# Quarter weights in partition order, and the second token tile and first mask on ScalarE's queue, in the ramp of a block-sparse gated layer

## Chip, cores and metric

One core of a Trainium2 chip. The time is device microseconds of one execution; lower is better. The kernel before has a median of 439.04 us over three runs (438.39 to 439.83).

## What is computed

The input x holds 2 batches of 1024 tokens with 1024 features, in float32. Each token is normalised over its features, without scale or shift. The normalised tokens go through two products with 1024 x 1024 matrices: `s`, with a weight of which only those 32 x 32 blocks count whose integer mask has a positive sum, plus a bias; and `g`, a dense weight plus a sum of eight low-rank products whose coefficients per batch are a softmax of scores against eight keys, followed by SiLU. The result is `x + s * g`.

```python
bm = mask.reshape(Nb, BH, Kb, BW).sum(axis=(1, 3)) > 0
w = (weight.reshape(Nb, BH, Kb, BW) * bm[:, None, :, None]).reshape(N, K)
s = einsum('bsk,nk->bsn', xn, w) + bias
delta = einsum('be,bser,ero->bso', coeffs, einsum('bsi,eir->bser', xn, lora_down), lora_up)
g = silu(einsum('bsi,oi->bso', xn, W_org) + delta)
out = x + s * g
```

## The kernel before

Products are made in three float32r passes on PE (TensorE): every operand is split into a high part and the remainder (`_hi`, `_lo`), and high by high, high by low and low by high are added up in PSUM (lines 456, 459 and 460). For the first batch, tokens lie on the partitions of the result in eight tiles of 128; the weights lie in `slot` tiles of 512 columns, the tokens in `xgrp`. The second batch is computed with a scheme of seven block products (line 1395) from sums of blocks that are prepared meanwhile.

What matters here is the ramp, the first 25 us or so, in which nothing is in SBUF. To begin early, it works with a quarter of the columns of the sparse weight (256 of 1024, `NQ`) and token tile by token tile. The order of the work of PE, DVE (VectorE), ACT (ScalarE) and POOL (GpSimd) is written out by hand, in a block with `manual_schedule`: what is written first is issued first on each of these engines, and each of them works strictly in that order. DMAs are issued by the queue of the engine that is named, here `nc.sync` (SP, SyncE) for all loads of the ramp, in the order written.

The loads and their tiles:
- `x_load(i)`: token tile i, 128 rows of 4 KB. Tile 0 (`acc`) comes in two halves of 2 KB per row, tiles 1 to 3 (`raw`) and 4 to 7 (`xlate`) whole.
- `mask_load(q)`: two transfers of 512 KB into `ramp`, the mask of quarter q in an order in which four partitions hold one block row.
- `w_load(q, k0)`: four of the eight row blocks of the quarter weights, 512 KB, into `ramp`.

The work on PE's way to its first real product is this:
- `warm_up(13)`: filler matmuls (`warm`, line 676) that depend on no data.
- `x_stats`, `rstd_of`, `shift_of`: mean and variance of tile 0 by halves on DVE (line 149), the power on POOL (line 157), the shift on DVE (line 163); `x_norm_half`: normalisation on ACT (line 167).
- `x_turn(0, 0)`, `x_turn(0, 1)`: eight transposes on PE (`pt`, line 210).
- `warm_up(12)`: twelve more fillers.
- Meanwhile on DVE, in this order: statistics of tile 1, the sum over the mask's first half (line 257), the sum over half of the mask's second half, with the other half on ACT (line 255), the join (line 261) and the spread (line 265).
- `mask_apply_mm(0)`: eight tiny matmuls (`mp`, line 275) that expand the block mask; then the weights are multiplied by it (`w_mul`, line 590, on DVE and POOL), split (`w_hi` on ACT, line 593, `w_lo`, line 597), and the products begin (line 456).

The first loads are written so:

```python
x_load(0, 2)
x_load(1)
mask_load(0)
w_load(0, 0)
w_load(0, 4)
x_load(2)
mask_load(1)
```

Of the kernel before, what the change touches and what calls it, by code (L numbers as in the profile page):

```python
# [17 lines left out]
P = 128  # L18
# [4 lines left out]
NH = 512  # L23
NQ = 256
# [8 lines left out]
def kernel(  # L33
# [11 lines left out]
    wq: bass.AP,  # L45
    wu: bass.AP,
    biasT: bass.AP,
    out: bass.AP,
):

# [10 lines left out]
    nc = tc.nc  # L61
# [75 lines left out]
    def nat_tile(dt=F32):  # L137
        k = turns[0] % 3
        turns[0] += 1
        v = raw_flat[:, k * D : (k + 1) * D]  # L140
        return v if dt == F32 else v.bitcast(dt)
# [420 lines left out]
    mh = [ramp[:, q, :, :].bitcast(I32) for q in range(2)]  # L562
    wh = [ramp[:, 2 + q, :, :].rearrange("p a (k n) -> p (a k) n", n=NQ) for q in range(2)]
    xr = [acc[0]] + [nat_tile() for _ in range(3)]
# [3 lines left out]
    sums = {}  # L568
    squares = {}

    def x_load(i, parts=1):
        n = D // parts
        for h in range(parts):
            nc.sync.dma_start(xr[i][:, h * n : (h + 1) * n], x[i * P : (i + 1) * P, h * n : (h + 1) * n])

    def mask_load(q):
        for c in range(2):
            nc.sync.dma_start(mh[q][:, c, :], mask[2 * q + c])

    def w_load(q, k0):  # L580
        nc.sync.dma_start(
            wh[q][:, k0 : k0 + 4, :],
            wT[k0 * P : (k0 + 4) * P, q * NQ : (q + 1) * NQ].rearrange("(k p) n -> p k n", p=P),
        )

    def w_mul(q, k0, eng, n=2):

# [65 lines left out]

    with tc.manual_schedule(engines={mybir.EngineType.PE, mybir.EngineType.DVE, mybir.EngineType.Activation, mybir.EngineType.Pool}):
        x_load(0, 2)
        x_load(1)
        mask_load(0)
        w_load(0, 0)
        w_load(0, 4)
        x_load(2)  # L660
        mask_load(1)
        x_load(3)
        w_load(1, 0)
        w_load(1, 4)
        nc.sync.dma_start(bias_bc, bias.partition_broadcast(P))
# [838 lines left out]
        close(cm_t, cm_o0, cm_t2, cm_g, cm_o1)  # L1504


_ORDER = ["x", "xT", "mask", "wT", "bias", "worgT", "down", "up", "keysT", "wq", "wu", "biasT"]


def _layout(inputs):  # L1510
    import numpy as np

    a = {k: np.asarray(v) for k, v in inputs.items()}
    x = a["L0_attn_data"].reshape(B * S, D)

    mask = a["L0_attn_mask"].reshape(8, 4, 32, 32, 32).transpose(0, 3, 1, 2, 4).reshape(8, P, D)

    down = (
        a["L0_ffn_lora_down"].transpose(0, 2, 1).reshape(4, P, NKT, P).transpose(2, 1, 0, 3)
    )  # L1520
    return {
        "x": x,
        "xT": x.T,
        "mask": mask,
        "wT": a["L0_attn_weight"].T,
        "bias": a["L0_attn_bias"],
        "worgT": a["L0_ffn_W_org"].T,
        "down": down,
        "up": a["L0_ffn_lora_up"].reshape(E_ * R_, D),
        "keysT": a["L0_ffn_lora_keys"].T,  # L1530
        "wq": a["L0_ffn_Wq"],

        "wu": a["L0_attn_weight"].T.reshape(2, 4, P, 2, 4, P).transpose(4, 2, 3, 0, 1, 5).reshape(4, P, 16 * P),
        "biasT": a["L0_attn_bias"].reshape(NKT, P).T,
    }


# [23 lines left out]
```

## Time and profile before

| | |
|---|---|
| Median of three runs | 439.04 us (438.39 to 439.83) |
| The profiled execution | 439.54 us, span 437.8 us |
| PE busy | 430.3 us, 98% of the span |
| DVE, ACT, POOL busy | 305.2, 184.6, 78.9 us |
| Granted TensorE clock | 1.0 of full speed |
| DMA | 88.48 MB, mean 202 GB/s |
| SP's queue (q1) | 64.77 MB; ACT's queue (q10) 7.08 MB; POOL's (q0) 16.26 MB |

The span is what the profiler sees of the program; the execution's time has 1.7 us more around it. Busy times of PE come from records whose ends are modelled. A row of the timeline gives the start, the length, the engine, the line and what is written from what, and in brackets how long the engine had been idle and whose work ended that idle time. "L574" is line 574 of the kernel before.

### The profile page before, as it was taken

To read this page: it belongs to the slowest core of one execution; us is meant where nothing else is said; L and a number is where in the kernel's file an instruction comes from. 1 tells how busy PE (TensorE), PEld (TensorE's weight loads), DVE (VectorE), ACT (ScalarE), POOL (GpSimd) and SP (SyncE) were. 2 spreads that over 40 slices of the span, in tenths; PEclk is the share of its full clock that TensorE was granted. 3 is DMA by queue.
4 is the path that set the end of the run, shared out by engine and by line. 5 is a ranking of instruction groups with operands and counts; after the bars stand their busy time and mean duration, and the time that the engine had idled before them with its cause. 6 is when DMAs were issued, how large, how long until landed. Compare 5 with 4: busy or idle time off the path is not lost.

```text
span 437.8 us, 5768 instructions
## 1 busy us (share of the span) xinstructions
PE 430.3 (98%) x2029; PEld 358.2 (82%) x2029; DVE 305.2 (70%) x508; ACT 184.6 (42%) x312; POOL 78.9 (18%) x103
## 2 busy tenths in 40 slices
PE   7999999999999999999999999999999999999996
PEld 5899888888888878888888888788888888888885
DVE  5889977766626779888966978878647385374624
ACT  3787435354731222236333344466335233441510
POOL 3342210002320312143132130010020030002000
PEclk9999999999999999999999999999999999999999
DMA  7996706777796798994699876996292165228003
GB/s 255 389 349 208 218 25 222 231 248 218 261 273 190 240 281 287 322 331 144 187 267 290 247 212 178 360 257 186 66 199 96 52 140 149 96 50 206 34 1 121
DMA packets 46013, 88.48 MB, mean 202 GB/s; under 512 B 4624, under 2 KB 15136, under 8 KB 45984
## 3 DMA queue, kind: packets, MB, share of 16 engines
q1 hardware_dynamic: 30480, 64.77, 44.7%
q0 software_dynamic: 6624, 16.26, 16.1%
q10 hardware_dynamic: 8880, 7.08, 5.0%
q8 instruction: 16, 0.26, 0.2%
q14 instruction: 13, 0.11, 0.1%
HBM read 68.17 MB, written 19.93 MB: 201 GB/s over the span
## 4 chain that ended last, share of the span: by engine, by line
PE 84%; DMA 5%; issue 4%; DVE 2%; POOL 2%; ACT 1%; SPq 0%; ACTq 0%; POOLq 0%; DVEq 0%
PE acc_ps L1395 25%; PE acc_ps L460 11%; PE acc_ps L459 11%; PE acc_ps L456 11%; PE py L1395 10%; PE psv L1149 6%; PE psw L421 2%; PE psw L420 2%; PE psw L1149 2%; PE psw L422 2%; DMA stash<-in_x_dram 2%; DMA xs<-xv 1%; DMA raw<-xv 1%; PE warm L676 1%; DMA acc<-in_x_dram 1%
## 5 line engine op out<-in xcount | busy, mean ns | idle before, releaser
L1395 PE MATMUL acc_ps<-xw,ow 128*128 128x512 f32 (+1 forms) x492 | 112.2, 384 | 0.2 <-DVE xw L1220 0.2
L456 PE MATMUL acc_ps<-slot,xgrp 128*128 128x512 f32 (+1 forms) x288 | 106.6, 370 | 0.1
L1395 PEld LDWEIGHTS acc_ps<-xw,ow 128*128 128x128 f32 x492 | 90.8, 188 | 18.9 <-DVE xw L1220 0.6
L460 PE MATMUL acc_ps<-slot,xgrp 128*128 128x512 f32 (+1 forms) x288 | 105.6, 367 | 0.2 <-DVE xgrp L609 0.2
L459 PE MATMUL acc_ps<-slot,xgrp 128*128 128x512 f32 (+1 forms) x288 | 105.5, 366 | 0.2
L460 PEld LDWEIGHTS acc_ps<-slot,xgrp 128*128 128x128 f32 x288 | 54.3, 188 | 9.6 <-DVE xgrp L609 0.6
L459 PEld LDWEIGHTS acc_ps<-slot,xgrp 128*128 128x128 f32 x288 | 54.3, 189 | 9.4 <-DVE slot L438 0.5
L456 PEld LDWEIGHTS acc_ps<-slot,xgrp 128*128 128x128 f32 x288 | 54.3, 189 | 9.4 <-ACT slot L593 0.6
L1395 PE MATMUL py<-xw,ow 128*128 128x512 f32 x192 | 46.3, 389 | 0.0
L1395 PEld LDWEIGHTS py<-xw,ow 128*128 128x128 f32 x192 | 36.0, 188 | 7.5
L1263 DVE TENSOR_TENSOR ow<-raw,ow 128x1024 fp32r<-128x1024 f32 (+1 forms) x32 | 34.5, 1087 | 7.7 <-ACT ow L1262 7.5
L1262 ACT CAST ow<-raw 128x1024 fp32r<-128x1024 f32 (+1 forms) x32 | 29.5, 941 | 3.0 <-DVE raw L1256 1.8
L508 POOL DMA_DIRECT2D stash<-in_x_dram x16 | 14.4, 900 | 74.7 <-DVE stash L505 74.7
L1378 POOL DMA_DIRECT2D gate<-in_xT_dram x12 | 10.5, 908 | 94.0 <-DVE gate L1372 67.9
L430 ACT CAST slot<-wo 128x512 fp32r<-128x512 f32 x16 | 9.9, 619 | 37.3 <-DVE wo L427 32.9
L420 PE MATMUL psw<-cut,dhi 128*128 128x512 f32 x64 | 24.9, 389 | 0.0
L421 PE MATMUL psw<-cut,dhi 128*128 128x512 f32 x64 | 24.9, 389 | 0.0
L422 PE MATMUL psw<-cut,dlo 128*128 128x512 f32 x64 | 24.9, 389 | 0.0
L1439 DVE TENSOR_TENSOR py<-py,s 128x512 f32<-128x512 f32 x8 | 5.6, 698 | 27.3 <-ACT s L1402 27.3
L1256 DVE TENSOR_TENSOR raw<-raw 128x512 f32<-128x512 f32 x32 | 21.4, 688 | 0.8 <-DMA raw<-yu 0.3
L1248 DVE TENSOR_TENSOR raw<-raw,m_sb 128x1024 f32<-128x1024 f32 x8 | 9.7, 1221 | 16.3 <-DMA raw<-in_wu_dram 16.3
L505 DVE TENSOR_TENSOR stash<-stash,mine 128x512 f32<-128x512 f32 x16 | 11.1, 692 | 10.8 <-ACT mine L481 10.5
(211 smaller groups left out, 605.0 us busy)
## 6 DMA issues: line engine op xcount, KB each, us to landing
wo<-in_worgT_dram SPq DMA_DIRECT2D x24, 256.0 KB, 3.9
raw<-in_x_dram SPq DMA_DIRECT2D x11, 512.0 KB, 4.4
ds<-in_down_dram SPq DMA_DIRECT2D x16, 256.0 KB, 3.4
stash<-in_x_dram POOLq DMA_DIRECT2D x16, 256.0 KB, 5.1
raw<-in_wu_dram SPq DMA_DIRECT2D x8, 512.0 KB, 5.8
raw<-yu SPq DMA_DIRECT2D x8, 512.0 KB, 3.8
out_dram<-stash ACTq DMA_DIRECT2D x14, 256.0 KB, 4.1
misc<-xv SPq DMA_DIRECT2D x12, 256.0 KB, 5.0
```

What stands on the lines that cost most here:

```text
L420: nc.tensor.matmul(ps, lhsT=dhi[:, c, :], rhs=u[c][:, 0, :], start=c == 0, stop=False)
L421: nc.tensor.matmul(ps, lhsT=dhi[:, c, :], rhs=u[c][:, 1, :], start=False, stop=False)
L422: nc.tensor.matmul(ps, lhsT=dlo[:, c, :], rhs=u[c][:, 0, :], start=False, stop=c == 3)
L456: nc.tensor.matmul(ps, lhsT=xs[:, kt, 0, cols], rhs=w[:, kt, 0, wc], start=kt == 0, stop=False)
L459: nc.tensor.matmul(ps, lhsT=xs[:, kt, 0, cols], rhs=w[:, kt, 1, wc], start=False, stop=False)
L460: nc.tensor.matmul(ps, lhsT=xs[:, kt, 1, cols], rhs=w[:, kt, 0, wc], start=False, stop=kt == NKT - 1)
L508: nc.gpsimd.dma_start(res, x[at], accum_op=ALU.add)
L1149: nc.tensor.matmul(ps, lhsT=w[:, a, wl, c, :], rhs=u[:, ul, :], start=start and c == 0 and n == 0, stop=c == 1 and n == 2, skip_group_chec ...
L1256: nc.vector.tensor_tensor(raw[:, o], raw[:, a], raw[:, b], op)
L1262: nc.scalar.copy(o[:, a:b, 0], raw[:, a:b])
L1263: nc.vector.tensor_tensor(o[:, a:b, 1], raw[:, a:b], o[:, a:b, 0].bitcast(F32), ALU.subtract)
L1395: nc.tensor.matmul(ps, lhsT=o[:, a, wl, j, :], rhs=xw[j][:, m, xl, cols], start=start and j == 0 and k == 0, stop=j == 3 and k == 2, skip_ ...
```

## The change

A new input `wr` holds the first 512 columns of the sparse weight once more, laid out on the host so that a load of `w_load` reads one run of 4 KB for each partition; before, a partition's share came in four runs of 1 KB. The bytes are the same and go to the same places. `x_load` and `mask_load` get an argument for the issuing engine, and tile 1 and the two transfers of the first mask are issued by ACT's queue. They are the first three instructions on ACT. SP's queue holds, in this order, the two halves of tile 0, the two weight loads, tile 2 and everything behind it as before. The order of all other instructions on every engine is the same. Lines of the changed kernel behind the edits are two lower for the ramp.

```diff
-    def x_load(i, parts=1):
+    def x_load(i, parts=1, eng=nc.sync):
         n = D // parts
         for h in range(parts):
-            nc.sync.dma_start(xr[i][:, h * n : (h + 1) * n], x[i * P : (i + 1) * P, h * n : (h + 1) * n])
-
-    def mask_load(q):
+            eng.dma_start(xr[i][:, h * n : (h + 1) * n], x[i * P : (i + 1) * P, h * n : (h + 1) * n])
+
+    def mask_load(q, eng=nc.sync):
         for c in range(2):
-            nc.sync.dma_start(mh[q][:, c, :], mask[2 * q + c])
+            eng.dma_start(mh[q][:, c, :], mask[2 * q + c])
 
     def w_load(q, k0):
-        nc.sync.dma_start(
-            wh[q][:, k0 : k0 + 4, :],
-            wT[k0 * P : (k0 + 4) * P, q * NQ : (q + 1) * NQ].rearrange("(k p) n -> p k n", p=P),
-        )
+        nc.sync.dma_start(wh[q][:, k0 : k0 + 4, :].rearrange("p k n -> p (k n)"), wr[q, k0 // 4])
...
         x_load(0, 2)
-        x_load(1)
-        mask_load(0)
+        x_load(1, eng=nc.scalar)
+        mask_load(0, nc.scalar)
         w_load(0, 0)
         w_load(0, 4)
         x_load(2)
...
+        "wr": a["L0_attn_weight"].T[:, :NH].reshape(2, 4, P, 2, NQ).transpose(3, 0, 2, 1, 4).reshape(2, 2, P, 4 * NQ),
```

More of the change, by code (lines that the diff above doesn't have):

```diff
@@ L47 @@
     biasT: bass.AP,
+    wr: bass.AP,
     out: bass.AP,
@@ L1504 @@
         close(cm_t, cm_o0, cm_t2, cm_g, cm_o1)
-_ORDER = ["x", "xT", "mask", "wT", "bias", "worgT", "down", "up", "keysT", "wq", "wu", "biasT"]
+_ORDER = ["x", "xT", "mask", "wT", "bias", "worgT", "down", "up", "keysT", "wq", "wu", "biasT", "wr"]
 def _layout(inputs):
```

## The prediction

> **What bounds the kernel now.** I read the page's engine table first, then the waits of PE alone, then the chain of waits over the first 14 us, then the timeline of PE, DVE and ACT there, and last the DMA by windows. All times are microseconds from the start of the span.
>
> The engine table and the waits of PE (engine and line, what it waited for, total, times, longest):
>
> ```profile
> PE 430.3 (98%) x2029; PEld 358.2 (82%) x2029; DVE 305.2 (70%) x508; ACT 184.6 (42%) x312; POOL 78.9 (18%) x103
> ...
> PE pt L210 <- ACT acc L167: 1.5, 1, 1.5
> PE warm L676 <- DVE ones_r L97: 1.1, 1, 1.1
> PE acc_ps L460 <- DVE xgrp L609: 0.2, 1, 0.2
> PE acc_ps L1395 <- DVE xw L1220: 0.2, 1, 0.2
> ```
>
> PE is busy for 98% of the span and has only four waits that count. The longest, 1.5 us, is in front of the first transposes. After the ramp nothing makes PE wait more than 0.2 us, so whatever the change gains or loses before PE becomes continuous goes through to the end at its full size. Only the ramp has to be costed. Its chain of waits (start, length, what):
>
> ```profile
> 0.81 0.38 SPq L574
> 1.24 3.62 DMA acc<-in_x_dram
> 4.89 0.70 DVE st L149
> 6.10 0.58 POOL rstd L157
> 6.95 1.53 ACT acc L167 x2
> 8.52 0.66 PE pt L210 x4
> 9.18 2.75 PE warm L676 x12
> 11.93 0.30 PE mp L275 x8
> 12.47 0.43 DVE ramp L590
> 12.92 0.41 ACT slot L593
> ```
>
> The chain starts with the second half of the first token tile (x0, tile acc), lands at 4.86, and goes statistics, rstd, normalisation, transposes, twelve fixed filler matmuls, then the mask's expansion (mp). The mask comes in only at mp. The same stretch as instructions (start, length, engine, what, idle before and its releaser):
>
> ```profile
> 4.89 0.69 DVE L149 BATCH_NORM_STATS2 st<-acc 128x6 f32<-128x512 f32 x1 [0.67 <-DMA acc<-in_x_dram]
> 7.90 1.29 DVE L149 BATCH_NORM_STATS2 st<-raw 128x6 f32<-128x512 f32 x2 [0.99 <-DMA raw<-in_x_dram]
> 10.48 0.63 ACT L255 ACTIVATE ramp<-ramp 128x512 f32<-128x512 int32 x1 [1.38 <-DMA ramp<-in_mask_dram]
> 8.94 2.99 PE L676 MATMUL warm<-ones_r 128*128 128x512 f32 x12
> 12.47 0.75 DVE L590 TENSOR_TENSOR ramp<-ramp,mp 128x256 f32<-128x256 f32 x2 [0.53 <-ACT m_sb L282]
> ```
>
> So the landings are: x0's second half 4.86, the second tile (x1) 7.88, the mask's second half 10.46. The weights were there already when first used at 12.47: that wait ends on ACT, not on a DMA. DMA by windows (length, then the engines, granted clock, DMA share, GB/s):
>
> ```profile
> 1.80:3.50 1.70, 1.70 (x6) 1.32 (x5) 0.67 (x2) 0.00 (x0) 1.12 (x1) 1.00 0.92 288
> 3.50:6.00 2.50, 2.50 (x9) 1.96 (x7) 1.74 (x4) 1.28 (x1) 1.42 (x2) 1.00 0.83 165
> 6.00:7.90 1.90, 0.44 (x3) 0.09 (x2) 0.23 (x2) 0.95 (x2) 0.57 (x1) 1.00 0.99 379
> ```
>
> From 6 us on the DMA engines are full at 379 GB/s; before that there is a slow stretch of 165 GB/s. One queue, SP's, already fills them.
>
> **The change, part by part.**
>
> *Weights in 4 KB rows.* Four loads of 0.52 MB. The weight rows flow at 375 GB/s (10 to 12 us) and the 4 KB rows of x at 422 (14 to 15 us), so a load takes 1.40 against 1.24: 0.16 us less for each, two of them before the first product. Nothing on the path waits for weights, so 0 is taken. If that cover went, they would be worth 0.3.
>
> *Three issues on ACT.* SP's issues of 512 KB take 0.42 to 0.43 us, so ACT spends about 1.3. Its first work is a table load of 1.28 at 3.57, which waits for x0's first half, and after it ACT idles 2.10 before the normalisation. Cost 0; 1.3 without that cover.
>
> *Three issues off SP.* What is queued behind them on SP (weights, x2, the second mask) goes out about 1.3 us earlier. x2 is first read at 18.61 and the second mask at 19.17, neither after a wait for DMA, so no gain. SP's queue has eight completion counters in turn: the second mask's first load now waits for x1 instead of x0's first half; behind it on SP stand x3 and the second weights. In before mask loads took a median of 8.7 us from issue to landing, with all the loads ahead of them in the queue, so an issue up to 1.4 us later is hidden there. Cost 0.
>
> *x1 and the mask beside x0.* This is the price. ACT is free when PE and DVE are (first instructions at 1.12 and 0.90), so x1 is issued at about 0.9, before x0's second half (1.24). What two hardware queues do at once is seen at 126.8 to 127.4: a store that ACT issued at 123.96 stands beside SP loads issued at 121.88, 124.24 and 124.81.
>
> ```profile
> q10 hardware_dynamic: 75, 0.15, 65.6%
> q1 hardware_dynamic: 30, 0.07, 29.4%
> ```
>
> ACT's queue (q10) takes two thirds, SP's (q1) falls to less than one third, and the sum is no more than before. So I expect x1's 0.52 MB to be served between the two halves of x0. The lower bound of the delay of x0's second half is then 0.52 MB at 400 GB/s, 1.3 us. The upper one is x1's own landing in before: 1.05 MB were through at 7.88, and now x0's second half is last of the same 1.05 MB, 7.88 - 4.86 = 3.0 us. I take the middle, 2.1, because the slow stretch of 165 GB/s may or may not come back. Outside these bounds: if x0 keeps its place and the slow stretch goes, DVE's 0.67 of idle between the halves is gained (-0.7).
>
> At this place the Trainium skill speaks against the change: "DMA: Bandwidth & Descriptors", section "Issuing engines are not separate DMA queues", says that transfers from all issuers share the same 16 engines and interleave, so that a second issuer saves only sequencer time. The windows above agree (full at 379 GB/s from one queue). By the rule the delay is at least the 1.3; if ACT's queue brought bandwidth of its own, it would be none.
>
> *What the mask gives back.* In before PE stood 0.26 in front of mp, because the mask's sums ended at 11.82, 1.36 after its landing at 10.46. With x0 late, the fillers end late, and that 0.26 closes if the mask is there in time. In issue order x0a, x1, x0b, mask, weights, mask, 2.6 MB end with the mask's second half instead of 2.1: 0.52/0.39 = 1.3 us later, 11.8, sums done at 13.1. The fillers end at 11.5 + 2.1 = 13.6. The mask is not late, and PE's 0.26 is gained.
>
> *Sum:* + 2.1 - 0.26 = + 1.84 us at mp, and nothing behind mp has slack to take it back. The profiled execution took 439.54 (span 437.8 and 1.7 around it) and would take 441.4; the median of the runs shown is 0.5 lower, 439.04, so 440.9.
>
> **The rivals.** A difference of 0.3%, 1.3 us, is about what a measurement of this kernel can tell from no change.
>
> *A second loss on top.* Either the mask's second half also falls behind both weight loads (3.1 MB through instead of 2.1, at 0.39 MB/us 2.7 later: 13.2, sums at 14.5, mp 14.6 against 11.87: + 2.7), or PE loses its warm clock. For that: the opening thirteen fillers took 5.23, 0.40 each, the twelve at 8.94 took 2.99, 0.25 each, after an idle of 1.46; that idle grows to 3.6. Twelve at 0.40 cost 4.8 instead of 2.99, + 1.8 on 1.84 = + 3.7, 442.7. Against it: transposes stand between, and the granted clock is 1.00 throughout. The Trainium skill ("TensorE: Matmul & The Clock Gate", section "What's actually happening") puts the array back to half clock after an idle window of about 3.4 us; no idle so long is in this trace, and by the page 3.6 would be just enough.
>
> *Faster.* x0's halves keep their place (SP's two transfers are served before ACT's first) and the slow stretch, which follows on x1's first rows, no longer lies in x0's way. Then x0's second half lands by 4.2, and the chain gains 0.67 + 0.26 = 0.93: 438.1. It decides at a landing of x0 before 4.86 with the mask no later than 10.4. For it: ACT has never issued a DMA before 110 us, so its start is unseen. Against it: the 2.1 MB that end with the mask would have to pass with the weights beside them.
>
> *It makes no difference.* x0 late by 1.3 or less, without the slow stretch: + 1.0 or less, 439.0 to 440.0.
>
> **How the numbers follow.** The forecast (x0 behind x1) 0.48, of which 0.41 lie over + 1.3; the second loss 0.18; no difference 0.16; faster 0.18. The price of the faster case is only 0.2%. I still count 0.16 of its 0.18 as over 0.3%: the scatter of the runs (438.39 to 439.83) is as large, and one of PE's small waits of 0.2 lies in the ramp behind mp and may close too. So faster 0.16, slower 0.41 + 0.18 = 0.59, same 0.07 + 0.16 + 0.02 = 0.25. The range goes from the faster case, 438.1, to + 4.0, 443.0, a little over the second loss; it leaves out about 1 in 10 at each end. The likeliest case's own range is 440.0 to 441.7.
>
> **What would show it.** In the changed profile the second statistics of x0 should start at about 7.0 instead of 4.89, PE's idle before the first transposes should be about 3.6 instead of 1.46, x1's statistics should follow without a DMA wait, the idle in front of mp should be gone, and the matmuls from the first product on should be the same rows moved by about 1.8. It is wrong if x0's second statistics start at or before 4.9, if mp waits for the mask, or if PE shows new waits after 45 us.

## The result

The changed kernel takes 443.76 us (median of 6 runs, 443.60 to 445.33); the kernel before, run beside it, 439.65 (6 runs, 438.39 to 440.34). The ratio is 1.0097 (95% interval 1.0074 to 1.0121): slower by about 4.1 us. The forecast was slower by 1.84.

The profiled execution of the changed kernel took 445.33, 1.6 above the median of its kind, with a span of 443.6. In it every matmul from mp to 130 us comes 4.29 us later than its counterpart in the kernel before; two later stretches add 0.23 and 0.84, and 0.44 lies behind the last matmul. This execution is 5.8 longer than the profiled one of before, so 4.29 of its loss arise by mp. The waits of PE, changed kernel:

```profile
PE pt L211 <- ACT acc L168: 4.1, 1, 4.1
PE py L1393 <- DVE ow L1261: 0.6, 1, 0.6
```

The wait before the transposes has grown from 1.5 to 4.1. The ramp on PE in the kernel before (PEld is the weight load of a matmul):

```profile
7.82 1.36 PE L210 MATMUL pt<-ident,acc 128*128 128x128 f32 x8 [1.46 <-ACT acc L167]
11.76 0.36 PEld L275 LDWEIGHTS <-misc 128*128 128x128 bf16 x8 [0.26 <-issue]
11.87 0.34 PE L275 MATMUL mp<-r,misc 128*128 128x8 bf16 x8
```

The ramp on DVE and PE, changed kernel (timeline):

```profile
5.45 0.70 DVE L150 BATCH_NORM_STATS2 st<-acc 128x6 f32<-128x512 f32 x1 [2.97 <-DMA acc<-in_x_dram]
7.24 0.69 DVE L150 BATCH_NORM_STATS2 st<-acc 128x6 f32<-128x512 f32 x1 [1.10 <-DMA acc<-in_x_dram]
9.18 1.28 DVE L150 BATCH_NORM_STATS2 st<-raw 128x6 f32<-128x512 f32 x2
10.17 1.97 PE L211 MATMUL pt<-ident,acc 128*128 128x128 f32 x8 [4.09 <-ACT acc L168]
11.79 4.52 PE L674 MATMUL warm<-ones_r 128*128 128x512 f32 x12
16.14 0.27 PEld L276 LDWEIGHTS <-misc 128*128 128x128 bf16 x8 [0.27 <-issue]
16.14 0.36 PE L276 MATMUL mp<-r,misc 128*128 128x8 bf16 x8
```

Three differences to the rows of before make up the 4.27 us by which mp is late (16.14 against 11.87). x0's second statistics start at 7.24 instead of 4.89: 2.35. From the first transpose to the first of the twelve fillers it takes 1.62 (10.17 to 11.79) instead of 1.12: 0.50. From there to mp it takes 4.35 instead of 2.93: 1.42. The last two are the same work on PE, only slower. The windows of the changed kernel (PE, PEld, DVE, ACT, POOL, then granted clock, DMA share, GB/s) say why:

```profile
1.80:3.50 1.70, 1.70 (x6) 1.31 (x5) 0.67 (x2) 0.00 (x0) 1.12 (x1) 1.00 0.71 205
3.50:6.00 2.50, 2.50 (x9) 1.72 (x7) 0.55 (x1) 0.51 (x1) 1.42 (x2) 1.00 0.97 370
8.00:8.50 0.50, 0.00 (x0) 0.00 (x0) 0.33 (x2) 0.00 (x0) 0.05 (x1) 0.72 1.05 434
12.00:13.50 1.50, 1.50 (x5) 1.21 (x5) 1.06 (x5) 1.00 (x3) 0.00 (x0) 0.50 1.02 407
15.00:15.50 0.50, 0.50 (x4) 0.41 (x3) 0.00 (x0) 0.00 (x0) 0.00 (x0) 0.96 0.99 393
```

The granted clock falls to one half at 8.22 (that is what a mean of 0.72 over 8.0 to 8.5 means) and comes back at 15.04. The transposes and most of the twelve fillers lie in between: fillers that start 0.23 us apart at full clock start 0.43 apart here. The column prints 1.00 from the start of the span as well, although the first opening fillers start 0.43 apart too; until the clock has first risen, the pace of the fillers tells more than the column. And x0 is late because both queues run at once. From 3.5 to 5.4 us, the DMA queues of the changed kernel:

```profile
q10 hardware_dynamic: 120, 0.43, 60.8%
q1 hardware_dynamic: 136, 0.25, 34.3%
```

ACT's queue (4 KB rows of x1 and mask) and SP's (2 KB rows of x0) move nearly equal counts of packets, and so ACT's moves almost twice the bytes.

### The profile page after: what moved, and what is told of

It reads as the page before. It is cut to its first block, busy times and chain, and to the rows that moved or that the text cites. A ratio compares the mean times of both kernels' runs of the same rounds, so it can differ in the third digit from the quotient of the medians.

```text
span 443.6 us, 5768 instructions
## 1 busy us (share of the span) xinstructions
PE 432.5 (98%) x2029; PEld 359.5 (81%) x2029; DVE 305.2 (69%) x508; ACT 184.4 (42%) x312; POOL 79.0 (18%) x103
```

## The experiments

Theory A has two parts: x0 lands late because it shares the DMA engines with ACT's loads, and PE, left without work, loses its clock. The rivals are the weights' layout (B), late data other than x0, which would set the end whatever the clock costs (C), and a clock that falls whatever PE does (D).

**One half of the change at a time.** First the weight rows alone:

```diff
-        x_load(1, eng=nc.scalar)
-        mask_load(0, nc.scalar)
+        x_load(1)
+        mask_load(0)
```

> The changed kernel with all loads back on SP's queue in the old order; only the weights' 4 KB rows are left. Theory A (the first token tile shares the DMA engines with ACT's loads and lands 2.35 us later, and PE, idle for 4.1 us, then runs at half clock): both causes are gone, so 0 to 0.3 us less than before, x0's second statistics at 4.9, granted clock 1.00. Rival B (the new weight rows disturb the first loads): most of the + 4.1 us stays.

Measured: 439.65 against 439.26, ratio 0.9998 (0.9975 to 1.0021). x0's second statistics start at 4.89, mp at 11.79. The data was earlier, but it did nothing: x1's statistics started at 7.03 without a DMA wait (before: 7.90, with one), while mp waits behind the fixed fillers. Then the queues alone, from the changed kernel:

```diff
-        nc.sync.dma_start(wh[q][:, k0 : k0 + 4, :].rearrange("p k n -> p (k n)"), wr[q, k0 // 4])
+        nc.sync.dma_start(
+            wh[q][:, k0 : k0 + 4, :],
+            wT[k0 * P : (k0 + 4) * P, q * NQ : (q + 1) * NQ].rearrange("(k p) n -> p k n", p=P),
+        )
```

> The changed kernel with the weights read in 1 KB rows as before; only the move of the second token tile and the first mask to ACT's queue is left. Theory A: + 4.1 us against before as in the changed kernel, within 0.5; x0's second statistics at 7.2, the twelve fillers in 4.5 us. Rival B (weight rows): no loss, 439 to 440.

Measured: 443.79, ratio 1.0102 (1.0076 to 1.0128). Its timeline:

```profile
9.96 1.82 PE L211 MATMUL pt<-ident,acc 128*128 128x128 f32 x8 [2.92 <-ACT acc L168]
11.43 4.19 PE L677 MATMUL warm<-ones_r 128*128 128x512 f32 x12
```

The whole loss is the move to ACT's queue; B falls. In this profile the clock was at half for 3.4 us only (10.55 to 13.96, against 6.8 in the profile of the changed kernel), and mp is 3.6 late instead of 4.3. The execution took 443.62, close to the median of the changed kernel: this is likely its usual course, and its own profile the longer one. The mean granted clock of each run says the same: 6.8 us at half would leave at most 0.992 of a run of 442 us, the profiled run of the changed kernel has 0.990, and four of its five others have 0.993 to 0.995.

**The clock without the late tile, and the late tile without the clock.** The kernel before with fewer opening fillers, so that PE's idle is longer and no load is moved:

```diff
-NWARM = 13
+NWARM = 6
```

> The kernel before with 6 opening fillers instead of 13: no load is changed, but PE is idle for about 4.1 us before the first transposes, as in the changed kernel. Theory A: half clock afterwards, transposes and the twelve fillers 1.5 to 2.2 us longer, + 1.5 to + 2.0 us, with x0's second statistics still at 4.9. Rival C (the clock costs nothing by itself): no difference within 0.5 us.

Measured: 441.54, ratio 1.0055 (1.0033 to 1.0077), + 2.3 us.

```profile
7.51 1.97 PE L210 MATMUL pt<-ident,acc 128*128 128x128 f32 x8 [3.46 <-ACT acc L167]
9.14 3.75 PE L676 MATMUL warm<-ones_r 128*128 128x512 f32 x12
```

x0 was even 0.3 earlier here (second statistics at 4.58), yet transposes and fillers take 1.97 and 3.75 instead of 1.36 and 2.99. No load was changed. But this is not a clock that fell. The opening fillers and the first of the twelve start 0.43 apart, and the pace of 0.23 begins only at about 10.7: with six fillers the clock had not yet risen. The windows print 1.00 all the same, in the middle of the slow fillers too, and the waits of PE show a second loss:

```profile
9.00:10.00 1.00, 1.00 (x5) 0.90 (x4) 0.92 (x2) 0.51 (x2) 0.00 (x0) 1.00 1.08 379
PE acc_ps L456 <- ACT slot L430: 0.9, 1, 0.9
```

From the transposes to mp it takes 5.22 instead of 4.05, so the slow pace costs 1.17, under the 1.5 to 2.0 expected, and with x0 earlier mp comes 0.86 late. The mask's sums were done at 10.91 and mp came at 12.73, behind the fillers, so C falls for mp. The rest of the + 2.3 arises later: the matmuls are 0.85 late up to 150 us and 2.07 at 170, behind the wait of 0.9 for a weight (slot). So the run shows that slow transposes and fillers delay mp with no load moved; it does not show what one fall of the clock costs. The reverse, the changed kernel with more opening fillers:

```diff
-NWARM = 13
+NWARM = 29
```

> The changed kernel with 29 opening fillers instead of 13, so that PE is busy until about 9.7 us and the idle before the first transposes is about 0.5 us. Theory A: the granted clock stays 1.00, the twelve later fillers take 3.0 us instead of 4.5, and only the late tile is left: + 2.1 us against before, 441.7. Rival C (late data sets the end, the clock only fills a wait): + 4.1 us stays. Rival D (the clock falls whatever PE does before): the same.

Measured: 443.09, ratio 1.0087 (1.0062 to 1.0111), a miss: the clock stayed at 1.00 and the twelve fillers took 2.98, but 29 fillers lasted past the normalised tile (transposes at 10.72; 2.93 after the second statistics, as elsewhere, would be 9.98). mp came 2.46 late in this profile, whose execution (442.31) was the fastest of the four; what the median's + 3.8 holds beyond that is not shown. The count depends on when the clock first rises: here the first 14 fillers came 0.43 apart, in the profile of the changed kernel the first 8. So again with 24:

> The changed kernel with 24 opening fillers. With 29 the fillers ended only at 10.5 us, 0.5 us after the normalised tile was there, and the run kept + 3.8 us of the loss. With 24 they end at about 9.6. Theory A (late tile 2.3 us, half clock 1.9 us): granted clock 1.00, transposes at 10.0, product stream moved by 2.0 in the profile, 441.3 to 442. Rival C (late data sets the end): as the changed kernel, 443.5.

Measured: 441.90, ratio 1.0067 (1.0043 to 1.0090). The changed kernel with 24 opening fillers, timeline:

```profile
9.94 1.36 PE L211 MATMUL pt<-ident,acc 128*128 128x128 f32 x8 [1.33 <-ACT acc L168]
11.05 3.01 PE L674 MATMUL warm<-ones_r 128*128 128x512 f32 x12
13.90 0.36 PE L276 MATMUL mp<-r,misc 128*128 128x8 bf16 x8
```

Clock 1.00 over the ramp, transposes and fillers as in the kernel before, mp at 13.90: + 2.03. This is the late tile alone, and it is the mechanism of the forecast's sum. From the transposes to mp it takes 3.96, in the profile of the changed kernel 5.97: the clock's fall costs 2.0 there. D falls: with PE kept at work the clock stays up. It is not certain in every execution: seven of the eight have a mean clock of 0.998 or 0.999, the longest one (444.61) 0.994.

**Why x0 is late.** The changed kernel with x0 in one transfer of 4 KB rows:

```diff
-        x_load(0, 2)
+        x_load(0)
```

> The changed kernel with the first token tile loaded in one transfer of 4 KB rows instead of two of 2 KB rows. Theory A1 (the two queues take turns row by row, so 2 KB rows against 4 KB rows get a third of the bytes): x0 and x1 share evenly and x0 is whole after 1.05 MB, at about 5.5 us instead of 7.2; statistics done about 1.0 us earlier, idle before the transposes 3.0 us; 1.0 to 2.5 us less than the changed kernel, 441.3 to 442.7. Rival A2 (ACT's queue is favoured as such): x0 is whole only after most of ACT's 1.57 MB, at 7 us or later, and the statistics end later than in the changed kernel, since they start only then: 444 or more.

```profile
5.52 1.29 DVE L150 BATCH_NORM_STATS2 st<-acc 128x6 f32<-128x512 f32 x2 [3.05 <-DMA acc<-in_x_dram]
```

The whole tile is there at 5.5, when with 2 KB rows only its first half was (5.45) and the second followed at 7.24. With rows of equal length the bytes are near equal too, 1.04 MB on SP's queue and 0.91 on ACT's from 1.8 to 7.2 us. The queues take turns row by row, and the queue with the shorter rows gets fewer bytes (A1); ACT's queue is not favoured as such (A2 falls). The time did not follow: 443.48, ratio 1.0089 (1.0059 to 1.0119), runs from 441.02 to 445.43. PE was idle for 3.1 us, and in the profile the clock was at half from 7.8 to 14.65. The spread goes with the clock: the fastest run has a mean of 0.998 and the slowest, the profiled one, 0.990. That the clock's phase decides is not shown. With 20 opening fillers beside it:

> The changed kernel with x0 in one transfer of 4 KB rows, and 20 opening fillers so that PE's idle before the transposes is about 1.5 us. Theory A: full clock throughout; x0 is whole at 5.5 us and its statistics end 1.0 us earlier than in the changed kernel, so of the two parts of the loss the clock's is gone and the late tile's is 1.0 instead of 2.0: + 1.0 us, 440.2 to 440.9. Rival D (the clock falls on its own): 442 or more.

Measured: 441.57, ratio 1.0054 (1.0030 to 1.0078). The clock stayed at 1.00 and mp came at 12.90, + 1.03, as expected of the tile; the time is above the 440.2 to 440.9 expected. The last matmul is 2.08 later in this profile: nearly all of the rest is lost between 280 and 310 us, with a wait of PE on DVE's ow that the kernel before does not have.

**Versions meant to beat both.** All loads on SP but x0's second half, which ACT issues, so that x0's halves lie side by side and nothing else does:

```diff
-        x_load(0, 2)
-        x_load(1, eng=nc.scalar)
-        mask_load(0, nc.scalar)
+        nc.sync.dma_start(xr[0][:, :NH], x[0:P, :NH])
+        nc.scalar.dma_start(xr[0][:, NH:], x[0:P, NH:])
+        x_load(1)
+        mask_load(0)
```

> All loads on SP in the old order with the weights' 4 KB rows, but the second half of the first token tile issued by ACT instead of SP. Theory A: the halves go side by side with equal rows and nothing else in their way, both there at about 4.1 us; DVE's 0.7 us of idle between the halves goes and mp comes 0.7 us earlier: 438.3 to 438.8. Rival (the first rows take their time whatever issues them): x0 as before, 439.3.

Measured: 440.02, ratio 0.9997 (0.9979 to 1.0015). The tile is whole at 3.98, mp at 11.47 (- 0.40), but the end is not earlier. With the mask's first half also on ACT, behind x0's half:

> As the one before, and the first half of the first mask is issued by ACT as well, behind its half of the first token tile; SP has the first half of that tile, the second tile, the mask's second half and the weights. Theory A: x0's halves still go first, so the same gain, 438.3 to 438.8; the mask is not on the path, so nothing more. Rival (any second load on ACT takes from x0): + 0.5 to + 1.5, 440 to 441.

Measured: 439.61, ratio 1.0009 (0.9993 to 1.0024). The tile is whole at 3.89, mp at 11.38: a second load on ACT behind x0 takes nothing from x0. But the gain of 0.5 does not show in the time. In both the mask's sums end about 1 us before mp, so the twelve fillers are what mp waits for. With eight, in that kernel and in the one with the rows alone:

```diff
-NWARM2 = 12
+NWARM2 = 8
```

> The kernel with x0's halves side by side on SP and ACT and half of the first mask on ACT, with 8 instead of 12 fillers between the first transposes and mp. In the run before, the mask's sums ended at 10.5 us but mp came at 11.4, behind the twelve fillers. Theory A (the fixed fillers took the place of the data as what sets mp): mp 0.9 us earlier, at 10.5, the product stream 1.4 us earlier than in the kernel before: 438.0 to 438.6. Rival (gains in the ramp are taken back by later waits): 439.4, no change.

> Only the weights' 4 KB rows, all loads on SP, and 8 instead of 12 fillers before mp. With the rows alone the mask's sums ended at 10.9 us and mp came at 11.8. Theory A: mp at 10.9 to 11.0, product stream 0.9 us earlier: 438.4 to 438.9. Rival (later waits take it back): 439.4.

Measured: 439.32, ratio 0.9993 (0.9976 to 1.0010), and 439.59, ratio 1.0005 (0.9992 to 1.0018). mp came at 10.68 and 11.11, the stream behind it 1.2 and 0.8 us earlier than in the kernel before. In the medians nothing of it is left. The waits of PE in the first of the two, and in the second:

```profile
PE py L1395 <- DVE ow L1263: 0.6, 1, 0.6
PE acc_ps L457 <- ACT slot L431: 0.5, 1, 0.5
```

```profile
PE acc_ps L457 <- ACT slot L431: 1.0, 1, 1.0
PE py L1393 <- DVE ow L1261: 0.6, 1, 0.6
```

The matmuls are 1.20 earlier up to 130 us, 0.38 earlier at 170 and level at the end in the first; 0.77 earlier, then 0.63 and 1.30 later in the second. The rival "later waits take it back" fits both. But these waits, for weights (slot) and operands (ow) of later stages, need not come from being early: ow costs 0.6 in the changed kernel too, where PE is 4.3 late, and slot 0.9 with six opening fillers, where it is 0.85 late. The slot that PE waits for in the second profile is made by ACT, which stood before it for a load of the tile stash; the row in the kernel before, where PE did not wait, and here:

```profile
157.55 0.62 ACT L430 CAST slot<-wo 128x512 fp32r<-128x512 f32 x1 [4.45 <-DMA stash<-in_x_dram]
158.22 0.62 ACT L431 CAST slot<-wo 128x512 fp32r<-128x512 f32 x1 [5.08 <-DMA stash<-in_x_dram]
```

So there the time was set by the landing of a load. No run changed these loads, and why such waits stand in most of the other profiles and not in that of the kernel before stays open.

## Why the prediction was wrong

*Direction and place* were right: slower, by x0's landing, ahead of mp, with the weights' rows worth nothing (rows alone 0.9998).

*The late tile* was sized well, though not for the reason given. Forecast 2.1; measured 2.35 in the changed kernel and 2.1 in the profiles with queues alone and with 24 fillers. The prediction put x1's 0.52 MB between the two halves, from a window at 126.8 us in which ACT's queue moved 75 packets against 30. In the ramp the queues took turns row by row, with near equal counts, and about 1.04 MB of ACT's loads were through at 7.2 us, when x0 ended; why the window at 126.8 differs is not shown. But the slow stretch of 165 GB/s was not there: 3.5 to 6.0 ran at 370. More bytes at a higher rate came to about the same.

*The 0.26 that mp would gain* was mis-sized. From the first of the twelve fillers to mp it takes 2.93 in the kernel before and 2.85 with 24 opening fillers or with the rows alone: 0.08. The idle of 0.26 stood in front of the weight load of mp and was read as a wait for the mask. It was not: the changed kernel has the same idle, 0.27, although the mask's sums were done at 13.09, 3 us before.

*The clock* is the step that failed. The sum let the same PE work follow at the same speed, and the clock was a rival, in a case of 0.18. It costs 1.92 in the profile of the changed kernel (0.50 + 1.42; 2.0 against the profile with 24 fillers) and 1.45 with queues alone (0.35 + 1.10); the rival's own price, twelve fillers at 0.40, + 1.8, was about right. Both reasons against it were wrong: transposes in between do not help when the clock has fallen before they begin, and a granted clock of 1.00 in the kernel before says nothing of a longer idle, the less since the column prints 1.00 over the slow opening fillers too, whose 0.40 the prediction had at hand. The sum should have carried it once the idle that the sum itself gave was 3.6 us, more than twice any in the trace.

*"Goes through to the end at its full size"* does not hold in either direction. Losses were not taken back, but later waits often added to them: 1.03 at mp became 2.25 in the medians with x0 whole and 20 fillers, 0.86 became 2.3 with six fillers. The new wait of 0.6 for ow, behind 300 us, is such a one, and the prediction had named new waits behind 45 us as a sign that it is wrong. Of gains nothing was left: 1.2 us won in the ramp came to nothing.

The range ended at 443.0; + 4.0 on 439.04 was its upper end and + 4.1 the measured loss, from a median of before that was 0.6 higher in these runs.

## What to carry to other kernels

Where the first tile sets the pace, issue nothing beside it on a second queue: two hardware queues here took turns row by row, and the tile with the shorter rows fell behind. When a step makes PE idle longer, price the clock as well as the idle, and look for fillers that were sized to an old landing time. A ramp of a PE-bound kernel can lose time for the whole kernel, but time won there has to get past every later wait. And read a clock column against the pace of like matmuls before trusting it at the start of a span.

## What the runs showed of the hardware

The clock's fall needs less idle than expected. It fell at 8.22 in the changed kernel, 2.15 us after the last opening filler ended (6.07), and at 7.8 with x0 whole, 1.9 after (5.90). It stayed up with idles of up to 1.74 us before the transposes, and fell before them or during them in the three profiles with an idle of 2.9 or more in which it had risen. It was at half for 6.83 us or for 3.41, and the opening fillers went from 0.43 to 0.23 apart anywhere between 4.1 and 7.3 us. The Trainium skill ("TensorE: Matmul & The Clock Gate", section "What's actually happening") has a free-running window of about 3.4 us, which fits these lengths and the changing start; its condition of an idle window is too strict for these runs, since the stretch of 3.41 us before the fall at 8.22 still had PE busy for 1.27 of it.
